# Two graph layers over a 4096 x 4096 adjacency matrix: fp8 copies on GpSimd, and layer 1's sums cut into more and shorter runs

## The chip, the cores and the metric

One core of a Trainium2 chip runs the kernel. The metric is the device time in microseconds of one execution, as the median over the runs. The core has five instruction streams that run side by side and meet only at semaphores: TensorE (PE in the profile, its weight loads PEld), VectorE (DVE), ScalarE (ACT), GpSimd (POOL) and SyncE (SP). Each stream works in its own order. Sixteen DMA engines move data between HBM and SBUF; most of this kernel's transfers are issued from POOL's stream, the stores from SP's.

## The reference

`x` is 4096 x 64, `adj` a 4096 x 4096 matrix of zeros and ones with a density of 1/256.

```python
# layer 0
rank = cumsum(adj, axis=1); deg = rank[:, -1:]
k = minimum(deg, 100); pos = rank - (deg - k)
w = adj * where(pos > 0, 0.5 ** (k - pos), 0)
x = layernorm(x + w @ (x @ W0) + b0)
# layer 1
deg = clip(sum(adj, 1) + 1, 1)
h = (adj @ x + x) / deg
z = relu(concat([x, h]) @ W1 + b1)
x = layernorm(x + z / max(norm(z), 1e-12))
```

So each row of `adj` is used twice. In layer 0 an edge is weighted by one half to the power of the number of edges of its row to its right. In layer 1 the plain matrix is multiplied with the result `x1` of layer 0, and a row block of that product needs all of `x1`.

## The kernel before

**Tiles.** The rows of `adj` are cut into eight slabs `g` of 512 rows, the columns into eight tiles `k` of 512. A tile (g, k) is one load of 1 MB of fp32, which the DMA turns into bf16 on its way, `A[g][k]`, 128 partitions x 4 x 512. There are 64 tiles and 64 **steps**, in the order g = 0..7 and, inside a slab, k = 7..0 (`steps`, `when[g, k]` is the step of a tile). All engines but the DMA follow the order in which the program is written (`manual_schedule`, L86).

**A step** (loop at L559) works on one tile. Its parts, in the order in which they are written:

- POOL: hooks of this step (`split_x`, `load_x`, `add_b0`), then `load_next` (L102), which issues the load of the tile that comes six steps later. The pool `a16` has 23 buffers; a load waits until the buffer that it takes is free.
- PE: `count` (L260) of tiles of the next chunk (a chunk has one, two or four tiles), 4 matmuls a tile; at a chunk's last one DVE writes the counts `cs`. Then `weigh` (L286): 16 matmuls with `tri`, 16 with `mine`, into two PSUM tiles `v`; ACT turns the first into half of the weights `w` (L310), DVE the second (L311). There is one pair of `v`, so the next `weigh` waits for both.
- PE: `some_sums` (L370), up to `QUOTA` = 4 matmuls of layer 1 (below).
- PE and ACT: `spread` (L279) at the end of a chunk's counts.
- ACT or DVE: `keep_next` (L336), from step 9 on in all steps but a slab's first: half a tile (128 x 1024) of the tiles k = 7..4 of slabs 0 to 3 is copied to fp8 (exact for zeros and ones), on DVE in every fourth step (L344), else on ACT (L346). After both halves layer 1 reads the fp8 copy and the bf16 buffer is free.
- PE: `gather` (L316) of the step before: 4 matmuls that add `w` times `x` into `acc0`.
- In a slab's first step ACT copies the `acc0` of the slab before (`first_hT`, L424). Then hooks for PE and DVE: the slab before goes through layer 0's layernorm over the next eight steps: `first_pz` in its step 1, `first_y` and `first_mv` (the moments, DVE) in step 2, `first_r` and `first_x1` (DVE) in 4, `first_xl` in 5, `first_px` (PE) in 6, `first_pu` in 7, `first_c1` (DVE) in 8. `x1hl` holds the result of layer 0 in two fp16 parts.
- DVE: `evict_part` (L362), if a run of layer 1's sums has ended in this step.

**Layer 1's sums.** The product of slab g's tile k with `x1` can start once slab k is through layer 0 (`ready`, L358: step 8(k + 1) + 7) and the tile is there. Such a **group** is four matmuls of 128 x 512 (`second`, L329). `jobs` (L351) lists runs of groups that add up in one PSUM buffer, `acc1`; its tag has one buffer. At the end of a run the sum goes to SBUF as `part[g]`: copied the first time (L368), added later (L365). Before, ten runs with 27 groups are done with the steps.

**The end** (L736 on) first finishes layer 0 of slab 7 (`first_pz(L)` to `first_lo(L)`), which gives the last `x1`, and beside it does the groups that are left (`own(g, b0, b1)`, L594; b counts quarter tiles). For each slab, `last_hT` adds the sum in PSUM to `part[g]` on DVE; then pairs of slabs, `unit(5, 2)`, `unit(0, 1)`, `unit(4, 3)`, and slab 6 go through `last_pz` (PE), `last_z` (DVE), `last_sq` (ACT or DVE), `last_ss` (DVE), `last_rn` (POOL, a power), `last_y` (DVE, then an addition on POOL), `last_mv` (moments, DVE), `last_r` (POOL or DVE), `last_o` (ACT) and `store` (SP). Slab 7 has its groups last, in two halves of 256 rows (`own_half`, L599).

Of the kernel before, what the change touches and what calls it, by code (L numbers as in the profile page):

```python
# [9 lines left out]
F32 = mybir.dt.float32  # L10
# [14 lines left out]
P = 128  # L25
R = 512
# [14 lines left out]
def adj_resnorm_kernel(  # L41
# [287 lines left out]
    def second(acc, g, b, first, last):  # L329
        nc.tensor.matmul(acc, lhsT=x1hl[:, b, :], rhs=A[g][b // KB][:, b % KB, :], start=first, stop=last)  # L330
# [3 lines left out]
    kept = {}  # L334

    def keep_next(i):  # L336
        if not to_keep:
            return
        g, k, h = to_keep.pop(0)
        if h == 0:  # L340
            kept[g, k] = a8p.tile([P, KB, R], F8, tag="a8", name=f"a8_{g}_{k}")
        qs = slice(h * KB // 2, (h + 1) * KB // 2)
        if i % 4 == 3:
            nc.vector.tensor_copy(kept[g, k][:, qs, :], A[g][k][:, qs, :], saturate=False)  # L344
        else:
            nc.scalar.copy(kept[g, k][:, qs, :], A[g][k][:, qs, :], saturate=False)  # L346
        if h == 1:
            A[g][k] = kept[g, k]


    jobs = [(0, 0, 2), (1, 0, 2), (2, 0, 2), (3, 0, 3), (2, 2, 4), (0, 2, 4), (1, 2, 4)]  # L351
    jobs += [(4, 0, 4), (5, 0, 5), (6, 0, 3)]
    have = {g: 0 for g in range(NG)}
    acc1 = {}

    todo = [(g, b, b == k0 * KB, b == k1 * KB - 1) for g, k0, k1 in jobs for b in range(k0 * KB, k1 * KB)]

    def ready(i, g, b):  # L358
        k = b // KB
# [2 lines left out]
    def evict_part(g):  # L362
        acc = acc1.pop(g)
        if g in part:
            nc.vector.tensor_tensor(part[g], acc, part[g], ALU.add)  # L365
        else:
            part[g] = const.tile([P, R], F32, name=f"part_{g}")
            nc.vector.tensor_copy(part[g], acc)  # L368

    def some_sums(i, n):  # L370

        done = None
        while n and todo and done is None and ready(i, todo[0][0], todo[0][1]):
# [4 lines left out]
            have[g] = b // KB + 1  # L378
            n -= 1
            if last:  # L380
                done = g
        return done
# [121 lines left out]
    def run(i, engine):  # L504
        for fn, args in hooks.pop((i, engine), []):
            fn(*args)
# [84 lines left out]
    acc = {}  # L591
    a_half, b_half = slice(0, R // 2), slice(R // 2, R)

    def own(g, b0, b1):  # L594

        for b in range(b0, b1):
            second(acc[g], g, b, b == have[g] * KB, b == NB - 1)

    def own_half(rows, b0, b1):  # L599
        for b in range(b0, b1):  # L600
# [141 lines left out]
    def acc_of(g, tag, rows=R, name=None):  # L742
        return ps_a.tile([P, rows], F32, tag=tag, name=f"acc_right_{name or g}")

    acc.update({5: va[:, 0, :], 2: vb[:, 0, :], 1: va[:, 1, :], 4: vb[:, 1, :]})
    acc[0] = acc_of(0, "acc1")
    last = L * KB
    own(5, 20, 24)
    first_pz(L)
    first_y(L)  # L750
    first_mv(L)
# [16 lines left out]
    last_hT(2)  # L768
    first_pu(L)
    first_c1(L)  # L770

    u = unit(5, 2)
    last_pz(u)
    own(0, 24, NB)
    last_z(u)
    last_sq(u, True)
    last_hT(0)
    last_ss(u)
    last_rn(u, True)
    own(1, 16, NB)  # L780
    last_hT(1)
    last_y(u, True)
    own(4, 16, 24)

    v = unit(0, 1)
    last_pz(v)
    own(4, 24, NB)
    last_mv(u)
    last_r(u, True)
    last_z(v)  # L790
    last_sq(v, True)
    last_hT(4)
    last_ss(v)
    last_rn(v, True)
    last_o(u, 0, 8)
    store(u)
    acc[3] = acc_of(3, "acc0")
    own(3, 12, NB)
    last_y(v, True)
    last_hT(3)  # L800
    acc[6] = acc_of(6, "acc1")
    own(6, 12, 20)

    u = unit(4, 3)
    last_pz(u)
    last_mv(v)
    last_r(v, True)
    last_z(u)
    last_sq(u, True)
    last_o(v, 0, 8)  # L810
    store(v)
    own(6, 20, NB)
    last_ss(u)
    last_rn(u, True)
    last_hT(6)
    acc[L, 0] = acc_of(L, "acc0", R // 2, "7a")
    own_half(a_half, 0, NB // 4)

    v = unit(6)
    last_pz(v)  # L820
    own_half(a_half, NB // 4, NB)
    last_y(u, True)
    last_z(v)
    last_sq(v, False)
    last_ss(v)
    last_rn(v, True)
    half_hT(a_half)
    acc[L, R // 2] = acc_of(L, "acc1", R // 2, "7b")
    own_half(b_half, 0, NB // 2)
    last_mv(u)  # L830
    last_s(u)
    last_y(v, True)
# [69 lines left out]
```

## Time and profile before

| | us |
|---|---|
| runs (3) | 260.9, 259.87, 263.14; median 260.9 |
| the profiled execution | 260.26 |
| its span, first to last instruction | 258.4 |
| PE busy / DVE busy / ACT busy / POOL busy | 215.9 / 179.9 / 147.7 / 77.6 |
| moved by DMA | 37.37 MB written, 69.40 MB read from HBM |
| share of the chain of waits: PE, DMA, DVE, issue | 37%, 23%, 17%, 9% |

The mean granted clock of TensorE is 0.975 of full speed. Busy times are sums over the whole span; PE's ends are modelled, so its busy time is a little too long. The kernel has three stages with different limits (the stream of tiles at first, then the steps with layer 1's groups, then the end), so the shares of the whole span say little, and the prediction reads it stage by stage.

In the views below a line of the timeline is: start in us, length in us, engine, line of the kernel, operation, out<-in, and how many were merged; in brackets the idle time before it and what ended it. A line of waits is: engine, line and operation that waited, what it waited for, then us in total, number of times and the longest. A line of groups is: line, engine, operation, out<-in with shapes and number, then busy us and mean ns of one, then idle time before.

### The profile page before, as it was taken

How to read it: one execution, taken by the hardware profiler on the slowest of the kernel's cores; microseconds unless marked ns; L12 is line 12 of the kernel's file. 1: busy time of each engine (PE TensorE's matmuls, PEld its weight loads, DVE VectorE, ACT ScalarE, POOL GpSimd, SP SyncE). 2: the span in 40 equal slices, each digit the busy share in tenths (PEclk: the TensorE clock that was granted, in tenths of full speed). 3: DMA queues.
4: the chain of work that ended last, by engine and by line, in shares of the span. 5: the costliest groups of instructions: out<-in, count | busy, mean ns of one | idle time of the engine just before them, and what ended most of it. 6: DMA issues, size and time to landing. Idle time of an engine off the chain costs nothing.

```text
span 258.4 us, 7468 instructions
## 1 busy us (share of the span) xinstructions
PE 215.9 (84%) x3187; PEld 99.5 (39%) x3187; DVE 179.9 (70%) x471; ACT 147.7 (57%) x210; POOL 77.6 (30%) x129
## 2 busy tenths in 40 slices
PE   8496767679979996998889899998996989999920
PEld 2122224224424432442344234433442636646920
DVE  5666697796797696667957694668577555556773
ACT  5366666687878668656866575447444421064271
POOL 8655471051013240232122422130200000475640
PEclk9779999999999999999999999999999999999995
DMA  5999999999999999599899999996500000000111
GB/s 90 179 238 233 240 214 214 221 219 214 215 221 205 202 188 211 107 212 191 169 148 188 205 215 213 223 212 118 104 0 3 3 0 0 3 22 20 43 41 41
DMA packets 12241, 37.37 MB, mean 145 GB/s; under 512 B 2353, under 2 KB 3377, under 8 KB 12209
## 3 DMA queue, kind: packets, MB, share of 16 engines
q0 software_dynamic: 10128, 35.66, 69.8%
q1 hardware_dynamic: 2080, 1.25, 1.7%
q8 instruction: 25, 0.41, 0.6%
q14 instruction: 8, 0.06, 0.1%
HBM read 69.40 MB, written 1.05 MB: 273 GB/s over the span
## 4 chain that ended last, share of the span: by engine, by line
PE 37%; DMA 23%; DVE 17%; issue 9%; POOL 6%; ACT 6%; POOLq 0%; ACTq 0%; DVEq 0%
DMA a<-in_adjT_dram 23%; PE acc L321 7%; PE acc_part L330 6%; DVE w L311 4%; PE v L294 4%; ACT w L310 4%; PE acc_right L330 3%; PE cnt L264 3%; PE v L303 2%; DVE x L459 2%; POOL a L111 2%; PE pz L640 2%; PE va L330 2%; PE pu L487 2%; PE vb L330 2%
## 5 line engine op out<-in xcount | busy, mean ns | idle before, releaser
L310 ACT ACTIVATE w<-v,less 128x1024 int16<-128x1024 f32 x64 | 71.3, 1114 | 48.3 <-PE v L303 30.1
L311 DVE TENSOR_SCALAR w<-v 128x1024 int16<-128x1024 f32 x64 | 78.2, 1222 | 29.3 <-PE v L303 27.5
L111 POOL DMA_DIRECT2D a<-in_adjT_dram x65 | 37.2, 574 | 111.7 <-PE acc_part L330 36.5
L321 PE MATMUL acc<-w,xhl 128*128 128x512 bf16 x256 | 66.3, 381 | 0.2 <-ACT hT L426 0.2
L321 PEld LDWEIGHTS <-xhl 128*128 128x128 f16 x256 | 24.0, 98 | 36.6 <-issue 12.8
L294 PE MATMUL v<-a,tri 32*32 32x512 bf16 x1024 | 29.7, 390 | 6.3 <-ACT w L310 5.9
L264 PE MATMUL cnt<-a,pick 128*32 128x512 bf16 x256 | 22.9, 393 | 12.6 <-DMA a<-in_adjT_dram 12.2
L330 PEld LDWEIGHTS <-x1hl 128*128 128x128 f16 x224 | 19.6, 98 | 29.3 <-issue 10.4
L303 PE MATMUL v<-near,mine 32*32 32x512 bf16 x1024 | 29.0, 382 | 0.2 <-ACT near L284 0.2
L274 DVE TENSOR_TENSOR cs<-cnt,cs 128x512 bf16<-128x512 f32 x22 | 15.1, 688 | 18.5 <-PE cnt L264 18.5
L330 PE MATMUL acc_part<-a,x1hl 128*128 128x512 bf16 x108 | 28.0, 382 | 0.0
L284 ACT ACTIVATE near<-rep,most 128x512 bf16<-128x512 f32 x30 | 20.5, 683 | 6.6 <-PE rep L282 6.6
L346 ACT CAST a<-a 128x1024 fp8e4<-128x1024 bf16 x23 | 23.9, 1038 | 0.0
L294 PEld LDWEIGHTS <-tri 32*32 32x32 bf16 x1024 | 10.8, 88 | 28.9 <-issue 27.5
L282 PE MATMUL rep<-cs,further 128*128 128x512 bf16 x30 | 11.8, 392 | 9.8 <-DVE cs L274 7.4
L410 POOL TENSOR_TENSOR rn<-ss,power 128x8 f32<-128x8 f32 (+1 forms) x4 | 6.0, 1506 | 34.8 <-DVE ss L664 34.7
L264 PEld LDWEIGHTS <-pick 128*32 128x32 bf16 x256 | 5.3, 94 | 28.6 <-issue 19.4
L330 PE MATMUL acc_right<-a,x1hl 128*128 128x512 fp8e4 (+1 forms) x56 | 12.9, 379 | 0.0
L654 ACT ACTIVATE sq<-z 128x512 f32<-128x512 f32 x3 | 1.9, 630 | 17.2 <-DVE z L647 17.2
L419 DVE BATCH_NORM_STATS2 st_l<-y 128x6 f32<-128x64 f32 x60 | 9.0, 214 | 1.0 <-POOL y L684 0.8
L303 PEld LDWEIGHTS <-mine 32*32 32x32 bf16 x1024 | 9.3, 88 | 0.8 <-issue 0.7
L464 ACT CAST x1hl<-x 128x256 f16<-128x256 f32 x8 | 3.2, 405 | 10.6 <-DVE x L459 10.6
(135 smaller groups left out, 255.8 us busy)
## 6 DMA issues: line engine op xcount, KB each, us to landing
a<-in_adjT_dram POOLq DMA_DIRECT2D x63, 512.0 KB, 9.3
c<-in_x_quads_dram POOLq DMA_DIRECT2D x8, 128.0 KB, 11.8
x<-in_x_dram POOLq DMA_DIRECT2D x8, 128.0 KB, 9.3
out_dram<-o SPq DMA_DIRECT2D x8, 128.0 KB, 1.7
a<-in_adjT_dram POOLq DMA_DIRECT2D x2, 256.0 KB, 4.9
w_sb<-in_L_gnn_W_dram SPq DMA_DIRECT2D x4, 16.0 KB, 10.8
w_sb<-in_L_gnn_weight_dram SPq DMA_DIRECT2D x2, 16.0 KB, 6.2
b_sb<-in_L_gnn_bias_dram SPq DMA_DIRECT2D x1, 32.0 KB, 8.2
```

The source lines that it names most:

```text
L111: nc.gpsimd.dma_start(out=a[:, qs, :], in_=adjT[g, k][:, qs, :])
L264: nc.tensor.matmul(cnt[g][quarters[q], :], lhsT=pick[:, PW - 4 * k : PW - 4 * k + Q], rhs=A[g][k][:, q, :], start=first, stop=last,)
L274: nc.vector.tensor_tensor(new, cnt[g], cs[g], ALU.add)
L282: nc.tensor.matmul(pr, lhsT=further, rhs=cs[g], start=True, stop=True)
L284: nc.scalar.activation(near[g], pr, AF.Relu, bias=most, scale=-1.0)
L294: nc.tensor.matmul(v[e // 2][quarters[q], e % 2, :], lhsT=tri[quarters[e], :], rhs=A[g][k][quarters[e], q, :], start=True, stop=False,)
L303: nc.tensor.matmul(v[e // 2][quarters[q], e % 2, :], lhsT=mine[quarters[e], 4 * k + q, :], rhs=nr[quarters[e], :], start=False, stop=True,)
L310: nc.scalar.activation(w[:, 0:2, :], v[0], AF.Relu, bias=less)
L311: nc.vector.tensor_scalar(w[:, 2:4, :], v[1], -STEP * MAX_NEIGH, 0.0, ALU.add, ALU.max)
L321: nc.tensor.matmul(acc0[g], lhsT=xhl[:, b, :], rhs=w[:, q, :].bitcast(BF16), start=(k, q) == (NK - 1, 0), stop=(k, q) == (0, KB - 1),)
L330: nc.tensor.matmul(acc, lhsT=x1hl[:, b, :], rhs=A[g][b // KB][:, b % KB, :], start=first, stop=last)
L346: nc.scalar.copy(kept[g, k][:, qs, :], A[g][k][:, qs, :], saturate=False)
```

## The change

It does four things.

- **The fp8 copies go to POOL.** `keep_next(i)` is called ahead of `load_next` in the step, so that POOL issues it in front of the load; it starts at step 3, runs in every step, and only for a tile whose own step is past. All 32 halves are POOL's: steps 3 to 34.
- **Runs of layer 1.** `jobs` now names lists of tiles instead of a range, in an order by when `x1` is ready; 20 runs with 39 groups. The built program has groups in steps 15, 16, 23 to 26 and, from step 30 on, in every step but 36. Runs end in steps 15, 16, 24, 25, 26, 32 to 35, 40 to 43, 48, 50, 56, 58, 60, 62 and 63.
- **Eviction.** The first copy of a `part[g]` is made by ACT instead of DVE. The additions stay on DVE.
- **The end.** `own(g, *ks)` takes tiles. 17 groups are left there instead of 29, nine of them ahead of `own(5, 7)` (before: seven ahead of its counterpart). `acc[6]` and both halves of slab 7 get PSUM from `ps_v` (`vc`, `vd`) instead of `ps_a`; `unit(6)` is placed between `unit(0, 1)`'s moments and `unit(4, 3)`'s, and slab 7's `first_pu` and `first_c1` are moved from ahead of `unit(5, 2)` to behind `last_pz` of slab 6. The work of the units themselves is the same.

```diff
     def keep_next(i):
-        if not to_keep:
+        if i < 3 or not to_keep or when[to_keep[0][0:2]] >= i:
             return
...
-        if i % 4 == 3:
-            nc.vector.tensor_copy(kept[g, k][:, qs, :], A[g][k][:, qs, :], saturate=False)
-        else:
-            nc.scalar.copy(kept[g, k][:, qs, :], A[g][k][:, qs, :], saturate=False)
+        nc.gpsimd.tensor_copy(kept[g, k][:, qs, :], A[g][k][:, qs, :], saturate=False)
...
-    jobs = [(0, 0, 2), (1, 0, 2), (2, 0, 2), (3, 0, 3), (2, 2, 4), (0, 2, 4), (1, 2, 4)]
-    jobs += [(4, 0, 4), (5, 0, 5), (6, 0, 3)]
+    jobs = [(0, [0]), (1, [0])]
+    jobs += [(2, [0, 1]), (0, [1]), (1, [1])]
+    jobs += [(3, [1, 0, 2]), (0, [2]), (1, [2]), (2, [2]), (4, [2, 1, 0, 3])]
+    jobs += [(0, [3]), (1, [3]), (2, [3]), (5, [3, 2, 1, 0, 4]), (3, [3, 4])]
+    jobs += [(6, [4, 3, 2, 1, 0, 5]), (4, [4, 5]), (0, [4, 5]), (1, [4, 5]), (2, [4])]
...
             part[g] = const.tile([P, R], F32, name=f"part_{g}")
-            nc.vector.tensor_copy(part[g], acc)
+            nc.scalar.copy(part[g], acc)
...
             run(i, POOL)
+            keep_next(i)
             load_next()
...
-            if i > NK and i % NK:
-                keep_next(i)
...
-    own(5, 20, 24)
+    acc[4] = ps_a.tile([P, R], F32, tag="acc1", name="acc_right_4")
+    own(5, 5)
     first_pz(L)
...
-    own(5, 24, last)
-    own(2, 16, last)
-    own(0, 16, 20)
+    own(5, 6)
+    own(2, 5, 6)
+    own(0, 6)
+    own(1, 6)
+    own(4, 6)
+    acc[3] = ps_a.tile([P, R], F32, tag="acc0", name="acc_right_3")
+    own(3, 5)
     first_px(L)
     first_x1T(L)
-    own(0, 20, 24)
-    own(5, last, NB)
+    own(3, 6)
+    own(5, 7)
     last_hT(5)
-    own(2, last, NB)
+    own(2, 7)
     last_hT(2)
+    own(0, 7)
...
+    vc = ps_v.tile([P, 2, R], F32, tag="v", name="vc")
+    vd = ps_v.tile([P, 2, R], F32, tag="v", name="vd")
+    acc[6] = vc[:, 0, :]
+    own(6, 6, 7)
...
+    last_ss(w)
+    last_rn(w, True)
+    last_hT(6)
+    acc[L, 0] = vc[:, 1, a_half]
+    acc[L, R // 2] = vd[:, 0, a_half]
+    own_half(a_half, 0, NB // 4)
+
+    u, v, y = v, unit(6), w
+    last_pz(v)
     first_pu(L)
     first_c1(L)
+    own_half(a_half, NB // 4, NB)
     last_mv(u)
     last_r(u, True)
     last_z(v)
-    last_sq(v, True)
+    last_sq(v, False)
     last_o(u, 0, 8)
     store(u)
+    last_y(y, True)
     last_ss(v)
     last_rn(v, True)
     half_hT(a_half)
     own_half(b_half, 0, NB // 2)
+    u = y
     last_mv(u)
     last_s(u)
```

More of the change, by code (lines that the diff above doesn't have):

```diff
@@ L342, in keep_next @@
         qs = slice(h * KB // 2, (h + 1) * KB // 2)
-        if i % 4 == 3:
-            nc.vector.tensor_copy(kept[g, k][:, qs, :], A[g][k][:, qs, :], saturate=False)
-        else:
-            nc.scalar.copy(kept[g, k][:, qs, :], A[g][k][:, qs, :], saturate=False)
+        nc.gpsimd.tensor_copy(kept[g, k][:, qs, :], A[g][k][:, qs, :], saturate=False)
         if h == 1:
             A[g][k] = kept[g, k]
-    jobs = [(0, 0, 2), (1, 0, 2), (2, 0, 2), (3, 0, 3), (2, 2, 4), (0, 2, 4), (1, 2, 4)]
-    jobs += [(4, 0, 4), (5, 0, 5), (6, 0, 3)]
-    have = {g: 0 for g in range(NG)}
+    jobs = [(0, [0]), (1, [0])]
[3 more added lines that the diff above has]
+    jobs += [(6, [4, 3, 2, 1, 0, 5]), (4, [4, 5]), (0, [4, 5]), (1, [4, 5]), (2, [4])]
     acc1 = {}
-    todo = [(g, b, b == k0 * KB, b == k1 * KB - 1) for g, k0, k1 in jobs for b in range(k0 * KB, k1 * KB)]
+    todo = [(g, k * KB + q, (k, q) == (ks[0], 0), (k, q) == (ks[-1], KB - 1)) for g, ks in jobs for k in ks for q in range(KB)]
+    left = {g: [k for k in range(NK) if not any(g == j and k in ks for j, ks in jobs)] for g in range(NG)}
     def ready(i, g, b):
@@ L377, in some_sums @@
             second(acc1[g], g, b, first, last)
-            have[g] = b // KB + 1
             n -= 1
@@ L592, in adj_resnorm_kernel, with own @@
     a_half, b_half = slice(0, R // 2), slice(R // 2, R)
-    def own(g, b0, b1):
-        for b in range(b0, b1):
-            second(acc[g], g, b, b == have[g] * KB, b == NB - 1)
+    def own(g, *ks):
+        for k in ks:
+            assert k in left[g]
+            for b in range(k * KB, (k + 1) * KB):
+                second(acc[g], g, b, b == left[g][0] * KB, b == NB - 1)
     def own_half(rows, b0, b1):
@@ L740, in adj_resnorm_kernel @@
     vb = ps_v.tile([P, 2, R], F32, tag="v", name="vb")
[L742 to L747, printed above, removed]
-    own(5, 20, 24)
+    acc.update({5: va[:, 0, :], 2: vb[:, 0, :], 0: va[:, 1, :], 1: vb[:, 1, :]})
+    acc[4] = ps_a.tile([P, R], F32, tag="acc1", name="acc_right_4")
+    own(5, 5)
     first_pz(L)
@@ L758, in adj_resnorm_kernel @@
     first_least(L)
-    own(5, 24, last)
-    own(2, 16, last)
-    own(0, 16, 20)
+    own(5, 6)
[5 more added lines that the diff above has]
+    own(3, 5)
     first_px(L)
     first_x1T(L)
-    own(0, 20, 24)
-    own(5, last, NB)
+    own(3, 6)
+    own(5, 7)
     last_hT(5)
-    own(2, last, NB)
+    own(2, 7)
     last_hT(2)
+    own(0, 7)
+    u = unit(5, 2)
+    last_pz(u)
+    last_hT(0)
+    last_z(u)
+    last_sq(u, True)
+    own(1, 7)
+    last_hT(1)
+    last_ss(u)
+    last_rn(u, True)
+    own(4, 7)
+    v = unit(0, 1)
+    last_pz(v)
+    last_hT(4)
+    last_z(v)
+    last_sq(v, True)
+    own(3, 7)
+    last_hT(3)
+    last_y(u, True)
+    last_ss(v)
+    last_rn(v, True)
+    vc = ps_v.tile([P, 2, R], F32, tag="v", name="vc")
+    vd = ps_v.tile([P, 2, R], F32, tag="v", name="vd")
+    acc[6] = vc[:, 0, :]
+    own(6, 6, 7)
+    w = unit(4, 3)
+    last_pz(w)
+    last_mv(u)
+    last_r(u, True)
+    last_z(w)
+    last_sq(w, True)
+    last_o(u, 0, 8)
+    store(u)
+    last_y(v, True)
+    last_ss(w)
[5 more added lines that the diff above has]
+    u, v, y = v, unit(6), w
+    last_pz(v)
     first_pu(L)
     first_c1(L)
[L772 to L787, printed above, removed]
+    own_half(a_half, NB // 4, NB)
     last_mv(u)
@@ L790, in adj_resnorm_kernel @@
     last_z(v)
-    last_sq(v, True)
-    last_hT(4)
-    last_ss(v)
-    last_rn(v, True)
+    last_sq(v, False)
     last_o(u, 0, 8)
     store(u)
[L797 to L824, printed above, removed]
+    last_y(y, True)
     last_ss(v)
@@ L827, in adj_resnorm_kernel @@
     half_hT(a_half)
-    acc[L, R // 2] = acc_of(L, "acc1", R // 2, "7b")
     own_half(b_half, 0, NB // 2)
+    u = y
     last_mv(u)
```

## The prediction

> **What bounds the kernel now.** I read the busy time by stage first, then TensorE's waits, then the timeline of a few steps. Stages are cut where a step's first `tri` matmul (L294) starts: step 16 at 64.4 us, step 24 at 84, step 30 at 103.5, step 40 at 134, step 48 at 159.6, step 56 at 183.1; the last `gather` ends at 204.4. Columns: stretch, length, then busy us of PE, PEld, DVE, ACT, POOL, granted clock, DMA share, GB/s.
>
> ```profile
> 64.40:84.00 19.60, 17.12 (x337) 7.75 (x347) 16.23 (x37) 16.06 (x21) 3.76 (x6) 1.00 1.07 214
> 84.00:103.40 19.40, 16.64 (x279) 6.69 (x278) 14.91 (x33) 13.62 (x17) 4.86 (x8) 1.00 1.05 201
> 103.40:134.00 30.60, 27.26 (x479) 12.06 (x475) 21.63 (x43) 20.55 (x25) 7.22 (x12) 1.00 0.88 163
> 134.00:159.50 25.50, 24.01 (x387) 10.28 (x383) 17.66 (x37) 14.92 (x18) 7.50 (x13) 1.00 1.03 204
> 159.50:183.00 23.50, 22.39 (x379) 9.59 (x375) 15.69 (x34) 12.18 (x15) 4.50 (x8) 1.00 0.87 172
> 183.00:204.40 21.40, 18.74 (x342) 8.56 (x339) 15.64 (x35) 11.53 (x14) 0.72 (x1) 1.00 0.14 31
> 204.40:258.40 54.00, 41.78 (x274) 26.54 (x272) 31.45 (x145) 17.87 (x46) 18.89 (x25) 0.94 0.06 20
> ```
>
> Up to step 30 the DMA share is over 1: the stream of tiles is the bound, and at 103.15 us TensorE still waits 2.0 us for tile 35. From step 30 on TensorE is the bound, with two kinds of holes. TensorE's own waits from 103.4 to 203 us:
>
> ```profile
> PE cnt L264 <- DMA a<-in_adjT_dram: 5.8, 5, 2.0
> PE v L294 <- ACT w L310: 3.7, 6, 1.6
> ```
>
> The first is the loads' fault: a load is issued six steps ahead, and from step 17 on the `a16` buffer that it takes was released only one or two steps earlier, by a copy or by a layer-1 matmul.
>
> **What the Trainium skill says.** "GPSIMD Engine Reference", section 3.1 Elementwise, gives a two-input operation about 2.6 cycles an element and one-input bodies 1.03 to about 1.8, at 1.2 GHz. The trace has two sizes of a two-input add:
>
> ```profile
> L684 POOL TENSOR_TENSOR y<-y,x 128x256 f32<-128x256 f32 x7 | 5.2, 756 | 4.0 <-DVE y L681 4.0
> L684 POOL TENSOR_TENSOR y<-y,x 128x128 f32<-128x128 f32 x1 | 0.4, 447 | 0.0
> ```
>
> That is 2.41 ns an element and 0.14 us fixed, near the page's 2.2 ns. No one-input copy on GpSimd is in the trace. "SBUF — State Buffer", section Who interferes with whom, says that a VectorE operation with two SBUF inputs and a GpSimd one that reads SBUF exclude each other. That concerns `xl` (L468, 0.41 us a slab); nothing in this trace shows it, and at most one copy a slab would be waited for, in the stage that DMA bounds.
>
> **Part 1, the copies.** ACT loses 23 x 1.04 = 23.9 us (L346), DVE 9 x 0.69 = 6.2 us (L344). POOL gets 32 copies of 128x1024, one ahead of the load in each of steps 3 to 34. Their price: half the two-input slope gives 1.2 ns x 1024 + 0.14 = 1.37 us, which I take; from below the page's 1.03 cycles, 0.88 us; from above the two-input slope, 2.61 us. At 1.37 a POOL step is 0.57 (load, L111) + 1.37 + (0.56 + 0.73)/8 for x and its bias = 2.1 us. A tile takes 0.524 MB at 208 GB/s (60 to 104 us) = 2.52 us, so copies up to 1.8 us are hidden by the stream. Steps 3 to 7 also have `xr` (0.68) and fall behind by 0.3 us each, covered by the 9.3 us from issue to landing. Queued behind a copy are the load, the x load and, to step 7, `xr`, for which DVE and then `gather` wait; the same slack covers these. What this buys: a load's buffer is free 5 to 13 steps earlier in program order, so the 5.8 us of waits go, but only from step 30, since before it the stream is saturated. Gain: 5.8 us. The freed ACT and DVE time is worth nothing by itself: in a step with layer-1 matmuls TensorE needs 2.42 us (133.98 to 136.40) and `w` on DVE 1.22.
>
> **Part 2, 39 groups in the steps instead of 27.** A group is four matmuls, 0.87 us (134.56 to 135.44). 134.0 to 159.5 has eight steps, all with a group, 1.8 us of DMA waits: 23.8 us, 2.97 a step. From step 30, 21 of the 34 remaining steps had a group; now 33 have (step 36 has none). Before: 34 x 2.97 - 13 x 0.87 + 5.8 + 13 x 0.42 = 101.0 (103.48 to 204.44; the 0.42 is what is left: a step with no group waits for `w`). After: 34 x 2.97 - 0.87 + 0.42 = 100.5, plus what follows.
>
> The runs are short, `acc1` has one buffer, and the next run mostly begins in the next step. Its first matmul now waits for the eviction, which stands last in its engine's step. Two places of the timeline show how late that is:
>
> ```profile
> 136.40 0.43 PE L294 MATMUL v<-a,tri 32*32 32x512 bf16 x16
> 136.50 0.59 ACT L426 COPY hT<-acc 128x512 f32<-128x512 f32 x1 [0.61 <-PE acc L321]
> 136.98 1.04 PE L330 MATMUL acc_part<-a,x1hl 128*128 128x512 bf16 x4
> ...
> 141.13 1.22 DVE L311 TENSOR_SCALAR w<-v 128x1024 int16<-128x1024 f32 x1
> 142.27 0.41 DVE L439 TENSOR_TENSOR y<-pz,x 128x256 f32<-128x256 f32 x1
> 142.60 0.15 DVE L440 TENSOR_SCALAR deg<-pz 128x4 f32<-128x4 f32 x1
> 142.72 0.60 DVE L419 BATCH_NORM_STATS2 st_l<-y 128x6 f32<-128x64 f32 x4
> 142.90 0.43 PE L294 MATMUL v<-a,tri 32*32 32x512 bf16 x16
> 143.24 0.36 DVE L421 BATCH_NORM_AGGREGATE mv_l<-st_l 128x2 f32<-128x6 f32 x4
> 143.48 1.04 PE L330 MATMUL acc_part<-a,x1hl 128*128 128x512 bf16 x4
> ```
>
> Runs of slabs 3, 4, 5, 6 end in steps 32, 40, 48, 56 and go to ACT (0.6 us) behind `hT`: free at 137.1 + 0.6 = 137.7 where TensorE asks at 136.98, a wait of 0.75. Runs ending in steps 34, 42, 50, 58 go to DVE (0.69) behind the first layer's moments: 143.6 + 0.7 = 144.3 against 143.48, 0.85. The run ending in step 60 stands behind `r` and `x1` (L400, L459; 1.76 us): 1.5. Sum 4 x 0.75 + 4 x 0.85 + 1.5 = **7.9 us**. Behind the waiting matmul on PE stand `gather`, the hooks and the next counts; behind the eviction, the next `w`. From below these waits could be nothing, if `gather` were late anyway; I take them whole, as PE has no other wait there once tiles are early. The other evictions (33, 41, 43, 62) lie behind a short queue and are hidden by `pz`, `px` or counts. DVE's additions rise from 3 to 13 and its copies fall from 7 to none, +6 x 0.69, beside PE.
>
> Last `gather`: before 204.4; now 103.5 + 100.5 + 7.9 = 211.9, **+7.5 us**.
>
> **Part 3, the end.** 12 groups less, 10.4 us of PE. I laid the new order out from the last gather (0), with durations of this trace: moments of 8 blocks 1.83, square on ACT 1.3, `ss` 0.93, `rn` 1.68, add 1.42, `r` with its offset 2.65. Slab 7's own chain is ready at 7.1 as before and now has eight groups beside it; `own(5, 7)` starts at 9.2 (before 8.3). Then pz(5_2) ends at 13.6, z 14.5, square 15.9, ss 16.9, rn 18.7, y and add 21.2, moments 23.1, z(4_3) 23.9, square 25.3, ss 26.3, hT(6) 27.0. TensorE is idle from 21.5 to 27.0: `own_half` writes the PSUM tile `vc` that hT(6) still reads, and the built program makes its first matmul wait for hT(6). Then eight half matmuls 28.0, pz(6) 28.8, pu 29.7, c1 30.7, moments(0_1) 32.5, POOL r(0_1) 35.3 and add(4_3) 36.8, moments(4_3) 38.6, its root 40.4, slab 7a to ss 41.4, moments(6) 42.3, POOL r(6) 44.3, add(7a) 44.8. From there to the end is unchanged: 7.95 us (250.46 to 258.4). End at 52.8, before 54.0: **-1.2 us**. TensorE's 10.4 us come back as waits for DVE, ACT and POOL, which take turns. The eight stores on SP only change places.
>
> **Sum.** +7.5 - 1.2 = +6.3 us on a span of 258.4. The profiled execution took 260.26 (1.9 outside the span), so 266.6 on its own time. That lies 0.6 under the median of 260.9, within the runs' spread; I forecast **266.5**.
>
> **Rivals.** (A) The evictions cost nothing and the end stays bound by TensorE. For it: PE is busy 41.8 of the last 54 us, and matmuls may start later than I have them. Against it: the queues above. Waits gone: 266.5 - 7.9 = 258.6; the end shorter by half of the other 9.2 us that I gave back: **254**; all of it, 249.4. (B) GpSimd copies too slow. The point is 1.8 us; at 2.61 a POOL step takes 3.35, 0.83 more than a tile, and over the 21 loads to tile 30 the stream loses 17 us, of which the 9.3 in flight cover half: +8, **274**. For it: POOL is slow here (1.67 us for eight powers). Against it: one input. (C) The change not doing what it says: the built order has the copies on POOL and 33 groups from step 30, so no chance is kept for it.
>
> **Numbers.** My forecast 0.55 (262 to 271), A 0.28, B 0.17. A measurement of this kernel tells about 2% from no change, 255.7 to 266.1. The forecast is split by that line, 0.25 within and 0.30 over it; A 0.16 faster and 0.12 within; B slower. Faster 0.16, same 0.37, slower 0.47. Range 254 to 274: it ends at the middles of A and B, whose outer halves, with the forecast's edges, are about 0.2.
>
> **What would show it.** Right: the last gather at about 212, no DMA wait of `cnt` after step 30, waits of `acc_part` for DVE and ACT of about 8 us, a TensorE gap of some 5 us ahead of `own_half`, DMA done by about 175 us. Wrong: copies over 1.8 us and DMA share under 1 before step 30 (B), or a gather end near 204 and an end of 45 us after it (A).

## The result, and the profile after

| | before | after |
|---|---|---|
| median of the runs, us | 261.2 (4 runs beside it) | 278.4 (277.27 to 278.71) |
| ratio | | 1.066, 95% interval 1.060 to 1.071 |
| span of the profiled execution | 258.4 | 275.5 |
| first `tri` matmul (L294) of step 8 | 35.7 | 35.8 |
| of step 9 | 39.1 | 46.4 |
| of step 13 | 52.5 | 58.9 |
| of step 14 | 56.4 | 66.2 |
| of step 17 | 64.4 | 77.0 |
| of step 30 | 103.5 | 113.4 |
| end of the last `gather` | 204.4 | 221.4 |
| from there to the end | 54.0 | 54.1 |

The change makes the kernel 17 us slower. A few executions of a kernel fall into a slower state; the medians here and below leave them out. (The last `gather` is taken to end where the next matmul starts. Steps count from 0. The one that starts at 64.4 us before is step 17; the prediction and the first expectations call it 16, while their 74.3 after is step 16 itself.) Three differences add up to the 17.1 us of the spans: +9.9 up to step 30, +7.0 from there to the last gather (107.95 us after, 100.96 before), +0.2 in the end. The forecast had 0, +7.5 and -1.2.

Where the first came from is read from the busy time by stage. Before, in the columns of the prediction (stretch, length, busy us of PE, PEld, DVE, ACT, POOL, granted clock, DMA share, GB/s), cut at steps 8, 9, 13, 14 and 17:

```profile
35.70:39.10 3.40, 2.12 (x45) 0.76 (x42) 3.23 (x10) 2.03 (x3) 1.90 (x4) 1.00 1.07 216
39.10:52.50 13.40, 9.84 (x184) 4.39 (x180) 10.35 (x25) 8.81 (x12) 1.58 (x3) 1.00 1.06 218
52.50:56.40 3.90, 2.52 (x56) 0.93 (x56) 3.76 (x12) 2.93 (x5) 3.38 (x6) 1.00 1.07 216
56.40:64.40 8.00, 7.59 (x141) 3.48 (x141) 5.68 (x9) 6.43 (x9) 1.14 (x2) 1.00 1.06 213
```

After, the same view, cut at the same steps, and the end:

```profile
35.80:46.40 10.60, 3.38 (x46) 0.91 (x42) 10.35 (x13) 2.24 (x3) 10.60 (x15) 0.73 1.06 213
46.40:58.86 12.46, 10.11 (x185) 4.41 (x181) 10.13 (x23) 6.75 (x10) 6.82 (x10) 0.95 1.07 220
58.86:66.20 7.34, 2.26 (x45) 0.80 (x45) 7.20 (x12) 1.90 (x4) 7.34 (x11) 0.89 1.06 214
66.20:77.00 10.80, 10.78 (x158) 4.23 (x157) 5.69 (x9) 6.10 (x8) 4.15 (x7) 0.76 1.06 219
...
221.40:275.50 54.10, 36.04 (x226) 25.27 (x224) 31.11 (x145) 17.88 (x46) 19.18 (x25) 0.82 0.06 20
```

Two single steps lose the time: 8 to 9 takes 10.6 us instead of 3.4, 13 to 14 takes 7.4 instead of 3.8. In both, DVE is busy nearly all the time with 12 or 13 instructions, and POOL is busy all the time. DVE had hardly any time to spare in these two steps before either: it was busy 3.23 of 3.40 and 3.76 of 3.90 us. The DMA share stays at 1.06: the stream of tiles is not starved, TensorE falls behind it. In and behind each long step the granted clock is low (0.73 in 35.8 to 46.4, 0.76 in 66.2 to 77.0). In the latter stretch PE is busy all of 10.80 us with work that, one group less, took 7.59 before, and steps 14 to 17 take 2.7 us more. Without the additional group, in the run of section 3, they still take 2.0 us more. From step 17 to 30, 36.5 us against 39.1, 2.6 come back: TensorE waited 2.4 us for tiles there before, and waits for none now.

The timeline of the first long step shows DVE, POOL and the TensorE instruction that waits (start, length, engine, line, operation, out<-in):

```profile
35.81 2.02 DVE L234 TENSOR_SCALAR wn_sb<-wn_sb 64x64 f32<-64x64 f32 x1
...
36.16 1.05 POOL L344 CAST a<-a 128x1024 fp8e4<-128x1024 bf16 x1
...
37.13 0.53 POOL L111 DMA_DIRECT2D a<-in_adjT_dram  x1
37.66 1.06 POOL L344 CAST a<-a 128x1024 fp8e4<-128x1024 bf16 x1
37.75 1.19 DVE L235 TENSOR_SCALAR w_sb<-w_sb 64x128 f32<-64x128 f32 x1
38.67 0.53 POOL L111 DMA_DIRECT2D a<-in_adjT_dram  x1
38.97 1.37 DVE L237 CAST w_parts<-w_sb 128x128 bf16<-128x128 f32 x1
...
40.37 1.01 DVE L239 TENSOR_TENSOR w_sb<-w_sb,w_parts 128x128 f32<-128x128 f32 x1
...
43.49 1.22 DVE L311 TENSOR_SCALAR w<-v 128x1024 int16<-128x1024 f32 x1
43.63 0.59 PE L282 MATMUL rep<-cs,further 128*128 128x512 bf16 x1 [7.22 <-DVE cs L274]
```

The same preparation before the change:

```profile
35.55 0.23 DVE L237 CAST w_parts<-w_sb 128x128 bf16<-128x128 f32 x1
35.81 0.29 DVE L239 TENSOR_TENSOR w_sb<-w_sb,w_parts 128x128 f32<-128x128 f32 x1
...
37.60 0.38 PE L282 MATMUL rep<-cs,further 128*128 128x512 bf16 x1 [1.28 <-DVE cs L274]
```

A copy and a load issue follow each other on POOL every 1.5 us. DVE's preparation of the second layer's weights, 0.2 to 0.4 us an instruction before (L234 193 ns, L237 282, L239 293 on average), now takes 1.0 to 2.0 us in each of its first five instructions. `w` (L311), which reads PSUM, takes its usual 1.22. No view calls this a wait: the time counts as DVE's busy time, and only a duration that is too long for its shape gives it away. `cs` (L274) stands behind these in DVE's queue, and TensorE waits 7.2 us for it. At step 13 the same happens to slab 0's `r` (L400, 2.32 us) and `x1`; TensorE then waits 5.1 us for `w`.

From step 30 to the last gather, TensorE's waits after:

```profile
PE acc_part L330 <- DVE part L366: 4.2, 5, 1.4
PE acc_part L330 <- ACT part L369: 2.3, 4, 0.6
```

The waits for tiles are gone, and 6.5 us of waits for evictions are there instead. In the end, the timeline has TensorE's gap ahead of `own_half`, DVE's wait for `pu` behind it, and a second gap:

```profile
247.33 1.87 PE L601 MATMUL vc<-a,x1hl 128*128 128x256 bf16 x8 [4.62 <-DVE hT L612]
248.99 1.81 PE L640 MATMUL pz<-wn_sb,hT 128*128 128x64 f32 x8
250.59 1.49 PE L487 MATMUL pu<-w_parts,x1T 128*128 128x128 bf16 x12
...
252.32 0.42 DVE L496 TENSOR_TENSOR t<-pu,deg 128x256 f32<-128x256 f32 x1 [5.05 <-PE pu L490]
...
260.76 1.12 PE L640 MATMUL pz_7a<-wn_sb,hT 128*128 128x64 f32 x4 [4.00 <-ACT hT L619]
```

### The profile page after: what moved, and what is told of

Same layout as the page of the kernel before. It is cut to its first block, busy times and chain, and to the rows that moved or that the text cites. A ratio compares the mean times of both kernels' runs of the same rounds, so it can differ in the third digit from the quotient of the medians.

```text
span 275.5 us, 7485 instructions
## 1 busy us (share of the span) xinstructions
PE 222.9 (81%) x3187; PEld 102.7 (37%) x3187; DVE 189.7 (69%) x465; ACT 131.3 (48%) x194; POOL 107.3 (39%) x161
## 3 DMA queue, kind: packets, MB, share of 16 engines
HBM read 69.40 MB, written 1.05 MB: 256 GB/s over the span
## 4 chain that ended last, share of the span: by engine, by line
PE 55%; DVE 25%; DMA 8%; ACT 5%; issue 3%; POOL 2%; ACTq 0%; DVEq 0%; POOLq 0%
PE acc L321 14%; PE acc_part L330 12%; DMA a<-in_adjT_dram 8%; PE v L294 6%; DVE w L311 5%; PE cnt L264 5%; PE v L303 3%; DVE cs L274 3%; PE pz L432 2%; PE pu L487 2%; DVE x L459 2%; DVE st_l L419 2%; ACT w L310 2%; PE va L330 2%; PE rep L282 2%
## 5 line engine op out<-in xcount | busy, mean ns | idle before, releaser
L311 DVE TENSOR_SCALAR w<-v 128x1024 int16<-128x1024 f32 x64 | 78.2, 1222 | 33.6 <-PE v L303 32.6
L321 PE MATMUL acc<-w,xhl 128*128 128x512 bf16 x256 | 68.1, 390 | 0.1
L111 POOL DMA_DIRECT2D a<-in_adjT_dram x65 | 35.5, 546 | 60.0 <-PE acc_part L330 36.6
L330 PE MATMUL acc_part<-a,x1hl 128*128 128x512 bf16 (+1 forms) x156 | 40.6, 382 | 7.1 <-DVE part L366 4.2
L321 PEld LDWEIGHTS <-xhl 128*128 128x128 f16 x256 | 25.0, 99 | 42.6 <-issue 17.2
L294 PE MATMUL v<-a,tri 32*32 32x512 bf16 x1024 | 30.3, 398 | 7.7 <-ACT w L310 7.5
L330 PEld LDWEIGHTS <-x1hl 128*128 128x128 f16 x224 | 19.4, 98 | 38.9 <-issue 22.8
L344 POOL CAST a<-a 128x1024 fp8e4<-128x1024 bf16 x32 | 33.6, 1049 | 0.0
L303 PE MATMUL v<-near,mine 32*32 32x512 bf16 x1024 | 29.8, 394 | 0.4 <-ACT near L284 0.4
L274 DVE TENSOR_TENSOR cs<-cnt,cs 128x512 bf16<-128x512 f32 x22 | 15.1, 688 | 21.6 <-PE cnt L264 21.5
L410 POOL TENSOR_TENSOR rn<-ss,power 128x8 f32<-128x8 f32 (+1 forms) x4 | 6.0, 1503 | 56.1 <-DVE ss L664 56.1
L264 PE MATMUL cnt<-a,pick 128*32 128x512 bf16 x256 | 21.7, 395 | 2.9 <-DMA a<-in_adjT_dram 2.5
L294 PEld LDWEIGHTS <-tri 32*32 32x32 bf16 x1024 | 10.3, 88 | 32.2 <-issue 31.1
L254 POOL TENSOR_TENSOR x<-x,b_sb 128x256 f32<-128x256 f32 x8 | 5.8, 725 | 30.8 <-DMA x<-in_x_dram 30.8
L722 ACT ACTIVATE o<-y,off,r 128x64 f32<-128x64 f32 x20 | 6.9, 426 | 9.2 <-POOL off L702 9.2
L264 PEld LDWEIGHTS <-pick 128*32 128x32 bf16 x256 | 4.7, 94 | 17.1 <-issue 9.1
L601 PEld LDWEIGHTS <-x1hl 128*128 128x128 f16 x64 | 7.7, 121 | 6.5 <-issue 4.7
## 6 DMA issues: line engine op xcount, KB each, us to landing
x<-in_x_dram POOLq DMA_DIRECT2D x8, 128.0 KB, 10.6
w_sb<-in_L_gnn_W_dram SPq DMA_DIRECT2D x4, 16.0 KB, 10.6
```

The source lines that it names most:

```text
L264: nc.tensor.matmul(cnt[g][quarters[q], :], lhsT=pick[:, PW - 4 * k : PW - 4 * k + Q], rhs=A[g][k][:, q, :], start=first, stop=last,)
L274: nc.vector.tensor_tensor(new, cnt[g], cs[g], ALU.add)
L294: nc.tensor.matmul(v[e // 2][quarters[q], e % 2, :], lhsT=tri[quarters[e], :], rhs=A[g][k][quarters[e], q, :], start=True, stop=False,)
L303: nc.tensor.matmul(v[e // 2][quarters[q], e % 2, :], lhsT=mine[quarters[e], 4 * k + q, :], rhs=nr[quarters[e], :], start=False, stop=True,)
L311: nc.vector.tensor_scalar(w[:, 2:4, :], v[1], -STEP * MAX_NEIGH, 0.0, ALU.add, ALU.max)
L321: nc.tensor.matmul(acc0[g], lhsT=xhl[:, b, :], rhs=w[:, q, :].bitcast(BF16), start=(k, q) == (NK - 1, 0), stop=(k, q) == (0, KB - 1),)
```

## The experiments

The theories: **P**, a GpSimd copy and a VectorE operation from SBUF to SBUF exclude each other. **Q**, the loss is one of POOL's queue or of late loads. **R**, it comes from the order of runs and evictions. **E**, the end is held up by the PSUM tile that slab 7's first half shares with slab 6. What the runs gave, each "after" with one edit unless it says otherwise; step 9, 14 and 30 are starts, "gather" is the time from step 30 to the end of the last gather, "end" from there. The kernel before stood at 261.2 or 261.3 us beside most runs and at 262.4 beside the runs of sections 6, 7, 8 and 12:

| run | median us | ratio to before, interval | step 9 | step 14 | step 30 | gather | end |
|---|---|---|---|---|---|---|---|
| before | 261.2 | 1 | 39.1 | 56.4 | 103.5 | 101.0 | 54.0 |
| after | 278.4 | 1.066, 1.060 to 1.071 | 46.4 | 66.2 | 113.4 | 107.9 | 54.1 |
| copies on ACT | 270.0 | 1.033, 1.024 to 1.042 | 39.5 | 56.1 | 103.3 | 109.3 | 54.8 |
| copies as before | 266.1 | 1.018, 1.011 to 1.025 | 39.4 | 56.5 | 102.2 | 108.0 | 53.9 |
| before, copies on POOL | 265.3 | 1.016, 1.008 to 1.024 | 46.4 | 66.3 | 112.8 | 96.8 | 53.9 |
| copies from step 9 | 276.6 | 1.059, 1.053 to 1.065 | 45.3 | 67.4 | 114.2 | 107.9 | 53.9 |
| copies from step 13 | 272.7 | 1.039, 1.031 to 1.047 | 39.2 | 61.0 | 107.7 | 108.5 | 52.7 |
| preparation on ACT | 276.8 | 1.058, 1.049 to 1.067 | 42.8 | 66.4 | 113.0 | 108.0 | 53.8 |
| shorter copies | 276.3 | 1.053, 1.045 to 1.061 | 44.7 | 64.9 | 113.9 | 108.0 | 54.1 |
| early eviction | 271.0 | 1.037, 1.031 to 1.042 | 47.6 | 67.3 | 113.8 | 102.2 | 53.1 |
| other tile | 275.7 | 1.055, 1.049 to 1.062 | 47.7 | 67.8 | 115.3 | 107.9 | 52.2 |
| three edits | 262.1 | 1.004, 1.001 to 1.006 | 39.3 | 56.0 | 104.1 | 103.5 | 53.1 |
| before, copies early on ACT | 258.4 | 0.985, 0.979 to 0.991 | 39.3 | 56.0 | 104.0 | 98.3 | 53.9 |

**1. The copies on ScalarE**, all 32 at the change's places.

```diff
-        nc.gpsimd.tensor_copy(kept[g, k][:, qs, :], A[g][k][:, qs, :], saturate=False)
+        nc.scalar.copy(kept[g, k][:, qs, :], A[g][k][:, qs, :], saturate=False)
```

> The changed kernel with its 32 fp8 copies on ACT instead of POOL, at the same places of the program. Theory P (port): a copy on GpSimd keeps VectorE from starting any operation that takes its input from SBUF by the shared way, for one or two copies, and this is the 10 us lost in steps 8 to 16. Then step 16 starts at 64 to 66 us (74.3 in the changed kernel, 64.4 before), no short VectorE operation takes over 0.7 us there, and the time is 267 to 271 us. Rival R (order): the early start of the copies and the new order of buffers delay the loads; then step 16 stays at 72 or later and the time at 275 or more.

Step 30 comes at 103.3, as before: the whole loss ahead of it belongs to the engine that copies, not to the place of the copies in the program. A copy takes 1.05 us on either engine; L237 is back at 270 ns. 109.3 us from step 30 on show that the slower second part is not the copies' doing.

**2. The copies as before** (engines, places and first step), the rest of the change kept.

```diff
-        if i < 3 or not to_keep or when[to_keep[0][0:2]] >= i:
+        if not to_keep:
...
-        nc.gpsimd.tensor_copy(kept[g, k][:, qs, :], A[g][k][:, qs, :], saturate=False)
+        if i % 4 == 3:
+            nc.vector.tensor_copy(kept[g, k][:, qs, :], A[g][k][:, qs, :], saturate=False)
+        else:
+            nc.scalar.copy(kept[g, k][:, qs, :], A[g][k][:, qs, :], saturate=False)
```

> The changed kernel with the copies as before the change (ACT and DVE, behind spread, from step 9). What is left is the new list of runs and the new end. Theory P: 7.5 us more in the steps by the eviction queues, about nothing at the end: 267 to 271 us, with about 7 us of waits of acc_part for evictions. If late loads come back, 2 to 4 us more. Rival E (the end is the loss): steps as before, gather end near 205, and the end over 60 us.

The time lies just under the 267 to 271 us that were expected. The rest of the change alone costs 5 us at the median, all of it from step 30 on (108.0 against 101.0 us, less 1.3 us by step 30). There TensorE waits 4.2 us for DVE and 2.3 us for ACT in `acc_part`, the same as after, and for no tile, though the copies are as late as before.

**3. The kernel before, with only the copies on POOL** and at the change's places; runs, evictions and end are the old ones.

```diff
+            keep_next(i)
             load_next()
...
-        if i % 4 == 3:
-            nc.vector.tensor_copy(kept[g, k][:, qs, :], A[g][k][:, qs, :], saturate=False)
-        else:
-            nc.scalar.copy(kept[g, k][:, qs, :], A[g][k][:, qs, :], saturate=False)
+        nc.gpsimd.tensor_copy(kept[g, k][:, qs, :], A[g][k][:, qs, :], saturate=False)
```

> The kernel before with only the copies moved to POOL, as in the change. Theory P: step 16 at 74, 10 us lost, up to 5.8 us of load waits got back later: 263 to 271 us. Rival Q (the loss needs the new runs): step 16 at 64 to 66, 255 to 261 us.

The loss by step 30 is there, 9.3 of the 9.9 us (112.8), so runs and evictions have next to no part in it: R is out for this stage. Then the old runs take 96.8 us instead of 101.0: of the 5.8 us of waits for tiles, 4.2 come back.

**4. The disputed cost by itself.** A probe that leaves the kernel's whole computation out: on DVE six rounds of nine operations, first with POOL empty, then beside copies of 128x1024 back to back, beside copies and load issues in turn, beside load issues alone.

```diff
+        for _ in range(6):
+            nc.vector.tensor_scalar(t["ts"], big[:, 0:64], 2.0, None, ALU.mult)
+            nc.vector.tensor_tensor(t["tt"], big[:, 0:4], big[:, 4:8], ALU.mult)
...
+            nc.vector.tensor_copy(t["cast"], big[:, 0:128])
+            nc.vector.bn_stats(t["bn"], big[:, 0:64])
+            nc.vector.tensor_scalar(t["pw"], pb, -1.0, 0.0, ALU.add, ALU.max)
```

> A probe that leaves out the whole computation: nine forms of short VectorE operations, six times each, four times over: alone, beside a train of 45 GpSimd copies of 128x1024 bf16 to fp8, beside 24 such copies each followed by a load issue, and beside 24 load issues. Theory P: beside copies the forms that read only SBUF in two-input or fast one-input form wait, by 0.5 to 2 us each; forms that read PSUM alone (128x1024), reduce and bn_stats keep their time within 5%. Beside load issues alone nothing waits over 0.5 us. Rival Q (GpSimd's queue is late, VectorE is not held): all forms keep their time in all four.

Groups of the probe by form; the tiles are named after the part (`alone`, `copies`, `both` for copies and load issues in turn):

```profile
L101 DVE TENSOR_SCALAR pw_alone<-pb 128x1024 int16<-128x1024 f32 x6 | 7.2, 1207 | 0.0
L101 DVE TENSOR_SCALAR pw_copies<-pb 128x1024 int16<-128x1024 f32 x6 | 7.2, 1200 | 0.0
...
L99 DVE CAST cast_copies<-big 128x128 bf16<-128x128 f32 x6 | 5.1, 847 | 0.0
...
L95 DVE TENSOR_SCALAR ts_copies<-big 128x64 f32<-128x64 f32 x6 | 4.5, 756 | 0.0
...
L99 DVE CAST cast_alone<-big 128x128 bf16<-128x128 f32 x6 | 1.2, 196 | 0.0
...
L95 DVE TENSOR_SCALAR ts_alone<-big 128x64 f32<-128x64 f32 x6 | 1.1, 185 | 0.0
L97 DVE SCALAR_TENSOR_TENSOR stt_both<-big 128x4 f32<-128x4 f32 x6 | 4.9, 825 | 0.0
...
L97 DVE SCALAR_TENSOR_TENSOR stt_alone<-big 128x4 f32<-128x4 f32 x6 | 0.9, 156 | 0.0
```

Beside copies, `tensor_scalar` and the cast, which have one SBUF input, wait about 0.6 us on average (756 and 847 ns instead of 185 and 196). What reads PSUM waits for nothing, and neither do `bn_stats`, `reciprocal` and the reduction, which also have one SBUF input; beside load issues alone the first two take 186 and 205 ns. For two SBUF inputs the expectation was met only in part. `tensor_tensor` was not longer (148 ns); in five of the six rounds it follows at once on an operation that had waited. But the first DVE operation beside a new train of copies, one with two inputs, took 0.97 us, and in the kernel the first L239 takes 1.0. In the part with copies and load issues in turn the loads' landings held POOL up, so the two engines overlapped in few places. Where they did, in three of six rounds, `scalar_tensor_tensor` with two SBUF inputs took 1.45 to 1.56 us: each began during a load issue and ended with the copy behind it.

**5 and 6. The first copy at step 9, then (`i < 13` in the same line) at step 13.**

```diff
-        if i < 3 or not to_keep or when[to_keep[0][0:2]] >= i:
+        if i < 9 or not to_keep or when[to_keep[0][0:2]] >= i:
```

> The changed kernel with only the first fp8 copy on GpSimd moved from step 3 to step 9 (32 copies, now in steps 9 to 40). Theory P (a GpSimd copy and a VectorE operation from SBUF to SBUF wait for each other, so the loss falls where DVE has many such operations in a row): the first loss goes because the preparation of the second layer's weights and b1 (steps 7 and 8) is past: step 8 to 9 takes 3.4 to 4 us as before (10.6 in the changed kernel), step 9 comes at about 39.2. The second, at step 13 to 14 (r and x1 of slab 0, with copies beside them), stays at 6 to 7.5. Step 30 at about 106, the time 271 to 274. Rival (the late loads or POOL's own queue in the first steps, whatever DVE does): the loss moves with the copies, a step of 7 us or more comes right behind step 9, and step 30 stays near 113.

> The changed kernel with the first fp8 copy at step 13 of the program (32 copies in steps 13 to 44). With the first at step 9, GpSimd ran ahead of TensorE and its first copy began at 35.5 us, just as VectorE began the preparation, so nothing was told apart. At step 13 it begins some 8 us later, behind the preparation. Theory P: step 8 to 9 takes 3.4 to 4 us as before (10.6 in the changed kernel) and step 9 comes at 39 to 40; r and x1 of slab 0 still lie beside copies and cost 3 to 4 us more than before at step 13 to 14 or one step later; step 30 comes at 106 to 109 and the time is 271 to 275 (a little may be lost to buffers that come free later). Rival (the loss goes with GpSimd's copies wherever they begin): a step of 7 us or more comes right behind the first copies, and step 30 is at 112 or later.

With step 9, P's numbers were missed: step 8 to 9 takes 9.6 us instead of 3.4 to 4, and step 30 comes at 114.2. The trace has the first copy at 35.5 us. POOL runs ahead of TensorE, and its step 9 falls on DVE's preparation, which belongs to TensorE's steps 7 and 8. With step 13 the numbers of P came: step 9 at 39.2, step 30 at 107.7, 272.7 us. What loss is left has moved to slab 0's `x1`; the timeline of that kernel:

```profile
53.72 1.03 POOL L344 CAST a<-a 128x1024 fp8e4<-128x1024 bf16 x1
53.82 5.59 DVE L459 TENSOR_SCALAR x<-y,mv_l,r_l 128x64 f32<-128x64 f32 x4
...
54.70 0.57 POOL L111 DMA_DIRECT2D a<-in_adjT_dram  x1
...
60.97 0.64 PE L294 MATMUL v<-a,tri 32*32 32x512 bf16 x10 [5.07 <-ACT w L310]
```

Four operations of 0.31 us take 5.59 us in all, singly 0.98, 2.23, 1.16 and 1.47: each ends shortly behind the end of a copy. The subtraction `xl` behind them, with two SBUF inputs, takes 1.75 us instead of 0.42. ACT's `w` stands behind `first_hi`, which waits for `x1`, and TensorE behind both. This speaks against Q: POOL's work is the same, and the loss is where it meets DVE's.

**7. The preparation on ScalarE**: the one-input operations of L234 to L248.

```diff
-            nc.vector.tensor_copy(w1_parts[:, j, :], w1_sb)
+            nc.scalar.copy(w1_parts[:, j, :], w1_sb)
```

> The changed kernel with the one-input operations of the preparation for layer 1 (L234, L235, L237, L243, L248: scalings and casts of the weights and of b1, steps 7 and 8) on ScalarE instead of VectorE; the two-input subtractions stay on VectorE, the copies on GpSimd. Theory P: ScalarE doesn't wait for GpSimd's copies, so these operations take 0.2 to 0.4 us each and step 8 to 9 falls from 10.6 us to 4 to 6; step 13 to 14 (r and x1 on VectorE beside copies) stays at 7; step 30 comes at 107 to 110, the time is 272 to 275. Rival (GpSimd's copies slow every reader of SBUF, or the loss comes from loads that are issued late): the same operations are stretched on ScalarE too, step 8 to 9 stays at 9 or more, the time within 2 of 278.

The expectation came true in part. Beside the same copies, ACT's operations take 0.24 to 0.40 us (L237 0.30), and step 8 to 9 takes 5.4 us; the two-input subtractions left on DVE wait (L239 1.65 and 0.71 us against 0.29). The time is not the one expected: step 9 to 10 takes 7.6 us instead of 4.7 (b1's preparation now goes to and fro between ACT and DVE ahead of `cs`, which is the likely cause), and step 14 comes as late as after.

**8. Shorter copies**, two of 128x512 each.

```diff
-        nc.gpsimd.tensor_copy(kept[g, k][:, qs, :], A[g][k][:, qs, :], saturate=False)
+        for q in range(h * KB // 2, (h + 1) * KB // 2):
+            nc.gpsimd.tensor_copy(kept[g, k][:, q, :], A[g][k][:, q, :], saturate=False)
```

> The changed kernel with each fp8 copy on GpSimd cut into two instructions of 128x512, back to back, 64 instead of 32, the same elements. If a VectorE operation waits for the GpSimd instruction that is under way and then has its turn, the waits halve (about 0.5 us in place of 1.05): L237 falls from 854 ns to about 550, step 8 to 9 from 10.6 us to about 7, step 30 comes at 108 to 110, the time is 273 to 275. If it has no turn before GpSimd leaves off copying for a moment (2.0 to 2.5 us for one operation were seen, more than one copy), nothing gets better: L237 stays at 800 ns or more, step 30 at 113 or later, the time 277 to 281.

Between the two. L237 falls to 423 ns and step 8 to 9 to 8.7 us, but other operations wait longer (L248 1056 ns instead of 244, L239 976 instead of 654), a pair takes POOL 1.17 to 1.27 us instead of 1.05, and step 30 is no earlier. How DVE gets its turn is not settled by this.

**9. The eviction right behind `gather`**, ahead of `first_hT` and the hooks.

```diff
             held = (g, k, w)
+            if done is not None:
+                evict_part(done)
...
             run(i, DVE)
-            if done is not None:
-                evict_part(done)
```

> The changed kernel with only the eviction of a run moved: evict_part stands right behind the step's gather, ahead of first_hT and of the hooks of PE and DVE, so its copy or addition is the first thing that ACT or DVE does after w. Queue theory (the 7.1 us that acc_part waits for DVE and ACT from step 30 on come from what stands ahead of the eviction in its engine's queue, not from the eviction itself): the waits of acc_part fall below 2 us, the last gather comes at 214 to 217 instead of 221.4, the time falls by 4 to 7 us to 271 to 274. Length theory (one acc1 buffer, and 0.6 to 0.7 us of eviction between two runs wherever it stands, or a wait that only moves to hT and the next gather): the waits of acc_part or new waits of acc for hT stay at 5 us or more and the time is within 2 us of 278. Before step 30 nothing changes in either (step 30 at 113).

The queue theory holds: the waits of `acc_part` for DVE and ACT are gone, the stretch from step 30 takes 102.2 instead of 107.9 us, and the median falls by 7.4.

**10. Slab 7's halves in each other's tiles.**

```diff
-    acc[L, 0] = vc[:, 1, a_half]
-    acc[L, R // 2] = vd[:, 0, a_half]
+    acc[L, 0] = vd[:, 0, a_half]
+    acc[L, R // 2] = vc[:, 1, a_half]
```

> The changed kernel with only the PSUM places of slab 7's two halves exchanged: the first half is summed in vd, the second in vc, so the first half's matmuls no longer share a tile with slab 6's sum, which hT(6) reads. Theory E (hT(6) holds TensorE up only through the shared tile): the wait of 4.6 us of own_half for hT(6) goes; its eight matmuls (2.2 us) fill it, and what is left, some 2.4 us, is a wait of the slab 6 pz for hT(6). If TensorE is what bounds the end, the stretch from the last gather to the end falls from 54.2 by about 2 us to 52, the time to 276. Rival: the end is bound by the chain of DVE, ACT and POOL (hT(6) to pz, z, square, power, moments), and the end stays within 0.5 us of 54.2. The clock after the idle time is the third thing to see: if TensorE's slow matmuls behind the gap (pu 1.49, slab 7 pz 1.81) come from idling, they are faster here and the end falls by more than 2.

The end falls from 54.1 to 52.2, as expected; TensorE's waits in the end of this kernel:

```profile
PE pz L640 <- DVE hT L612: 3.8, 1, 3.8
```

The wait of `own_half` is gone, and slab 6's `pz` waits 3.8 us for hT(6) instead (2.4 were expected). The size of the gain is not settled by one trace: the runs that leave the end as the change has it show 52.7 to 54.8 us, and the same exchange in section 11 gives 53.1. That TensorE holds the end up here is seen more directly in the trace after, where DVE waits 5.05 us for `pu`. Step 30 came 1.9 us later in this trace, which the edit doesn't touch. That the slow matmuls behind the gap come from idling is not told apart by it, since a gap of 3.8 us stays.

**11. Three edits together**: the diffs of 1, 9 and 10.

> The changed kernel with three edits together: the 32 copies on ScalarE at the places that the change gave them, the eviction right behind gather, and slab 7's halves in exchanged PSUM tiles. If the three causes stand on their own, their gains add up: copies on ScalarE 270.0 measured, less 4 to 6 for the evictions (5.0 us of acc_part waits were left there), less 0 to 2 for the end: 262 to 266, no longer slower than the kernel before by a measurable amount. If the copies on ScalarE only trade one wait for another, 268 or more.

The gains add up: 262.1 us. New runs, better evictions and a better end only make up for what they cost: from step 30 to the last gather the kernel still takes 103.5 us, where the kernel before takes 101.0.

**12. The kernel before, copies early and on ScalarE.**

```diff
-        if not to_keep:
+        if i < 3 or not to_keep or when[to_keep[0][0:2]] >= i:
...
+        nc.scalar.copy(kept[g, k][:, qs, :], A[g][k][:, qs, :], saturate=False)
...
+            keep_next(i)
             load_next()
```

> The kernel before with only the copies moved to where the change has them, in front of the load and from step 3, all 32 on ScalarE; runs, evictions and end as before. Adding what was measured apart: up to step 30 as with the changed kernel's copies on ScalarE (103.3), from there to the last gather as with copies on GpSimd and the old runs (96.8, the load waits gone), about 1 more for the copies on ScalarE that fall into steps 30 to 34, the end 54: span 255, time 256 to 258, ratio to before 0.98 to 0.99. If the load waits after step 30 come back because ScalarE's copies come later than GpSimd's, 260 to 262.

The fastest of all: 258.4 us, 1.5% under before (0.9 to 2.1%), with the ratio that was expected. All waits for tiles after step 30 are gone; 2.7 us are gained there.

## Why the prediction was wrong, and where it was right

**Part 1 failed, in one step: "at most one copy a slab would be waited for, in the stage that DMA bounds".** It was measured at +9.9 us by step 30, of the 10.8 by which the sum was off (17.1 against 6.3). Two things were wrong in it. First, which operations wait. The prediction took one rule from the Trainium skill's "SBUF — State Buffer", Who interferes with whom (two SBUF inputs), and found only `xl`. The same section says that copies, casts and `tensor_scalar` on VectorE can run in two-port modes, then need the pair of ports that GpSimd uses, and that whoever comes second is blocked for the whole instruction of the other. This case agrees (196 to 847 ns for a cast, 185 to 756 for a `tensor_scalar`), except that one operation can lose more than one copy (last section). DVE has ten operations of these kinds in the preparation of steps 7 and 8 alone. The rule with two inputs was not applied in full either: it also covers four subtractions there (L239, L249) and slab 0's `r` (L397, L400), while `xl`, the only one named, takes 0.42 us after as before. Second, the cover. That the stage is one "that DMA bounds" was taken for room on the other engines. But from step 8 to 17 TensorE was busy 22.1 of 28.7 us before, 0.7 us a step to spare, and in the two steps that grew DVE had less than 0.2 us to spare in each. A wait of 7.2 us within one step cannot hide in that.

**The price of the copy** was 1.05 us where 1.37 was taken, near its lower end of 0.88. The stream had the room that the prediction gave it: its share stayed at 1.06, and rival B (274 us, the stream starved) comes nearest by its time alone, not by its mechanism.

**The gain of 5.8 us**: the waits for tiles went, as forecast. By themselves, with the old runs, the early copies gave back 4.2 us on POOL and 2.7 on ACT. With the new runs they gave nothing measurable: with the copies as before, these runs took the same 108.0 us from step 30 on and waited for no tile. The waits went with the new runs too, so that this term came out was luck; why the new runs remove them is open.

**Part 2 was right about the evictions**: 107.95 us from step 30 to the last gather against 108.4 forecast. The waits for evictions were 6.5 us against 7.9 (ACT 4 x 0.58 where 0.75 was taken, DVE 4.2 in five against 4.9), at the places named, and they go when the eviction is put ahead of the queue: rival A (the evictions cost nothing) is out.

**Part 3 was right in its mechanism and off in size**: the gap ahead of `own_half` was 4.62 us (5.5 forecast), but the end is 54.1 us instead of 52.8. The term that was mis-sized is the matmuls behind the gap. Eight half matmuls, `pz` of slab 6 and `pu` were given 2.7 us (27.0 to 29.7) and took 5.0 (247.3 to 252.3); hT(6) came 1.1 us earlier than forecast, which made up for part of it. `pz` of slab 6 takes 1.81 us there, where before the same eight matmuls took 1.10; the second line below is the stretch of these matmuls after the change, and the third number from its right is the granted clock:

```profile
238.99 1.10 PE L640 MATMUL pz<-wn_sb,hT 128*128 128x64 f32 x8 [0.30 <-DVE hT L612]
...
245.60:252.30 6.70, 4.97 (x31) 4.41 (x31) 1.52 (x4) 2.85 (x9) 4.34 (x6) 0.50 0.11 39
```

The Trainium skill's "TensorE: Matmul & The Clock Gate", Part 1, says that an array that has been idle runs at half its clock until it has been busy for some 3.4 us. The trace agrees: the granted clock is 0.50 in this stretch and 0.82 on average in the end (0.94 before), and behind the 7.2 us wait of step 8 a `gather` of four matmuls takes 1.91 us instead of 1.02. Durations from a stretch without gaps were too short behind one.

## What to carry to other kernels

Before work goes to GpSimd, look at what VectorE does at the same time, and at forms, not at busy shares: here casts and `tensor_scalar` from SBUF to SBUF waited, operations with two SBUF inputs waited in part, what reads PSUM didn't, and beside copies on ScalarE a cast kept its time (L237, 270 ns). A stage that another resource bounds gives cover only as far as the engine behind it has time to spare in each single step. An eviction that frees a single buffer belongs ahead of its engine's other work.

## What the runs showed of the hardware that was not expected

A blocked DVE operation can lose more than one copy. L400 took 2.32 us, over two copies of 1.05 us with a load issue of 0.5 us between them. L234 took 2.02 us: it began during a load issue and lasted over a copy and the next load issue. The profile counts this as busy time, so DVE's busy share rises and no wait appears. Cutting the copies in half shifted the waits and lessened them little: up to step 30 DVE was busy 84.5 us instead of 86.1, against 74.0 with the copies on ScalarE.
